# Moving the input loads of a hybrid block from ScalarE to SyncE, behind a small store

## The chip, the cores and the metric

The kernel runs on one core of a Trainium2 chip, in one launch. The metric is device time in microseconds (us). Times are given as the median of several runs with the lowest and the highest. Beside these there is one profiled execution, of which a trace shows each instruction of the engines: TensorE (PE, with its weight loads as PEld), VectorE (DVE), ScalarE (ACT), GpSimd (POOL) and SyncE (SP). An engine works off its own instructions in order and waits for others through semaphores. ACT and SP also issue DMA transfers, and these issues stand in the same order as the engine's other instructions. They appear in the trace as ACTq and SPq.

## What is computed

Four stages follow each other, each on its layer norm and with a residual sum. `x` is [4, 1024, 256] in float32.

```python
x = x + lru(_layernorm(x))     # linear recurrence over 1024 steps, then a two-layer GELU block and a layer norm
x = x + ffn(_layernorm(x))     # two gated branches, each keeps the 32 largest of 256 softmax scores per token
x = x + attention(_layernorm(x))  # 8 heads of 64, keys and values from a latent of 64
x = x + ffn(_layernorm(x))     # the same weights again
```

In `lru`, `u = einsum(x, W_in) + b_in` gives a real, an imaginary and an output part. The complex state `h[t] = lam * h[t-1] + gamma * u[t]` is scanned over time, and `out = Re(h) W_mid[0] - Im(h) W_mid[1] + o`. Then comes `y = gelu(out w1) w2 + out`, and its layer norm with gain `ln_g` and base `ln_b`. In `ffn`, a grouped convolution, batch norm, GELU and a linear layer give the logits; the weight matrix is `w_ffn`, the linear layers are `lin_t` with biases `linb`.

## The kernel before

The 4096 tokens stand in eight blocks of 512 (`NBLK`), two blocks per batch. Block `k` is one tile of 128 partitions by 4 by 256, 512 KB, and stays in SBUF for the whole kernel: `load_x` (L1040) fills it by one DMA. Two blocks of one batch hold its even and odd time steps, so that a scan runs over 512 columns.

The LRU stage (L1064 to L1116) is written out by hand:

- `lru.head` (L357) normalizes a block: statistics on DVE (L133, L134), a row of small DVE operations for the inverse root (L55 to L66, L136), scaling on ACT (L145), transposes on PE (L147), and a split into a rounded part on ACT and a rest on DVE (L160, L161). The results are the `xnt` tiles.
- `lru.tables` (L230) makes the sine and cosine tables by doubling, with one half on ACT (L272, L273) and the sums on DVE (L269 to L275).
- `lru.states` (L381) multiplies (`pu`, L170), evicts on ACT (`u`, L390) and scans on DVE (L402 to L416).
- `lru.output_weights` (L310) prepares the output weights: `gw` on ACT (L316), `pm` on PE (L320, L323), a split (L160, L161).
- `lru.outputs` (L422) makes `po` (L170, L437), evicts it as `ot` on ACT (L438), multiplies `pz` (L443), applies GELU on ACT (`zt`, L446), multiplies again (L452), adds on DVE (L455), transposes (`py`, L465), takes statistics and normalizes (`ly`, `yn` on ACT at L474); the gain, base and residual run on POOL (L472 to L484).
- `f1.head` (L501) is the head of the first feed-forward stage, with transposes and the convolution `pc` (L529). It stores turned inputs `tt` to DRAM through SP (L527), the first of them at 134.79 us.

A scheduler sets the order of instructions on each engine from the dependencies. `tc.issue_after(ins)` adds an edge for order without a wait: what is traced in the block stands behind `ins` on the engine of `ins`. A wait comes only from data. Each DMA is given one of eight semaphores in turn, and an issue waits until the DMA that had the same semaphore before is done.

The loads before the change: SP issues blocks 0 and 1. ACT issues the vector constants, the LRU weights (L217 to L225), and, behind instructions of its own, blocks 2 and 3 (behind `lru.xnt_first`, the first cast of `xnt`), `brow` (gain and base, behind the fourth eviction of `u`), and then blocks 4 to 7 together with `ffn_weights` (L984), behind the eighth eviction of `u`. `ffn_weights` loads `lint` (four DMAs), `wf` (one) and, three times in turn through one buffer, three copies of a row `v`. Each `v` is split into three bfloat16 parts by casts on ACT (L1020, L1023, L1025) and differences on POOL (L1021, L1024). The parts are `linb`, twice, and `bias`.

After the LRU stage come eight tiles of the first feed-forward stage with the attention weights (about 290 to 385 us), and then the attention stage. There score products (`sc`, L881), exponentials on ACT (L889), transposes (L900 on PE, or through DMA at L894) and value products (`pmo`, L925) of one head run beside the feed-forward tiles of later blocks. At the end, the second feed-forward stage has its own tiles (L1203).

Of the kernel before, what the change touches and what calls it, by code (L numbers as in the profile page):

```python
# [10 lines left out]
F32 = mybir.dt.float32  # L11
# [10 lines left out]
P = 128  # L22
B = 4
T = 1024
D = 256
# [3 lines left out]
NBLK = B * T // 512  # L29
# [143 lines left out]
def by_block(v):  # L173

    return [
        v[b * T : (b + 1) * T, :].rearrange("(q p r) d -> r p q d", p=P, r=CH)[r] for b in range(B) for r in range(CH)
    ]
# [796 lines left out]
def run(*gens):  # L974
    for g in gens:
        for _ in g:
            pass
# [6 lines left out]
def ffn_weights(nc, rp, cp, w, lint, lin_t, w_ffn, rows):  # L984
    vecs = w.vecs


    grp = cp.tile([P, 32], F32, tag="grp", name="grp")
    nc.gpsimd.memset(grp, 1.0)
    nc.gpsimd.affine_select(  # L990
        out=grp, in_=grp, compare_op=ALU.is_ge, fill=0.0, base=0, pattern=[[-4, 32]], channel_multiplier=1
    )
    nc.gpsimd.affine_select(
        out=grp, in_=grp, compare_op=ALU.is_ge, fill=0.0, base=3, pattern=[[4, 32]], channel_multiplier=-1
    )
    for s in range(2):
        for k in range(KD):
            nc.gpsimd.tensor_scalar(
                w.cw[:, k, s * 32 : (s + 1) * 32],
                grp,  # L1000
                vecs[:, V_CW + 2 * s + k : V_CW + 2 * s + k + 1],
                0.0,
                ALU.mult,
                ALU.add,
            )
    nc.gpsimd.memset(lint, 0.0)
    for s in range(2):
        for k in range(KD):
            r = k * 64 + s * 32
            nc.scalar.dma_start(lint[r : r + 32, s, :], lin_t[s, k * 32 : (k + 1) * 32, :])  # L1010
    nc.scalar.dma_start(w.wf, w_ffn)

    nc.gpsimd.memset(w.ones, 1.0)
    parts = [slice(32 * i, 32 * i + 32) for i in range(3)]
    for dst, at in ((w.linb[:, 0:D], 0), (w.linb[:, D : 2 * D], D), (w.bias, 4 * D)):
        v = rp.tile([P, D], F32, tag="v", name="v")
        nc.gpsimd.memset(v, 0.0)
        for i in range(3):
            nc.scalar.dma_start(v[32 * i : 32 * i + 1, :], rows[0:1, at : at + D])
        nc.scalar.copy(dst, v)  # L1020
        nc.gpsimd.tensor_tensor(v, v, dst, ALU.subtract)  # L1021
        for i in (1, 2):
            nc.scalar.copy(dst[parts[i], :], v[parts[i], :])  # L1023
        nc.gpsimd.tensor_tensor(v[parts[2], :], v[parts[2], :], dst[parts[2], :], ALU.subtract)  # L1024
        nc.scalar.copy(dst[parts[2], :], v[parts[2], :])  # L1025
# [3 lines left out]
def tile_kernel(ctx: ExitStack, tc: tile.TileContext, x_in, w_lru, vecs_in, rows, w_ffn, lin_t, w_attn, w_down, out):  # L1029
    nc = tc.nc  # L1030
# [9 lines left out]
    def load_x(engine, blk):  # L1040
        engine.dma_start(blocks[blk], by_block(x_in)[blk])
# [9 lines left out]
    w = Weights()  # L1051
    w.ident, w.vecs = ident, vecs
    w.wf = cp.tile([P, KD, D], F32, tag="wf", name="wf")
    lint = cp.tile([P, 2, D], F32, tag="lint", name="lint")
# [5 lines left out]
    f1 = Ffn("f1", tc, bp, x, w)  # L1060
# [3 lines left out]
    with ExitStack() as c1:  # L1064
        psum = Banks(c1.enter_context(tc.tile_pool(name="ps1", space=PSUM)), {"pu": 2, "po": 2, "py": 2, "pt": 2})

        brow = c1.enter_context(tc.tile_pool(name="brow", bufs=1)).tile([P, 2, D], F32, tag="brow", name="brow")
        lru = Lru(tc, c1, ident, vecs, brow, w_lru, psum)
        xb = [x[4 * k : 4 * k + 4] for k in range(NBLK)]
        xnt = [lru.head(xb[0])]  # L1070
        lru.tables(lambda: xnt.append(lru.head(xb[1])))
        with tc.issue_after(lru.xnt_first):
            for blk in range(2, 4):
                load_x(nc.scalar, blk)
        h = [[lru.states(xnt, c) for c in range(KD)]]
        lru.output_weights()
        with tc.issue_after(lru.evacuated[3]):
            nc.scalar.dma_start(brow.rearrange("p a b -> p (a b)"), rows[0, 2 * D : 4 * D].partition_broadcast(P))
        xnt += [lru.head(xb[k]) for k in (2, 3)]
        h.append([lru.states(xnt[2:4], c) for c in range(KD)])  # L1080
        for k in range(NBLK):
            last = k >= NBLK - 2
            if k == 0:
                with tc.issue_after(lru.evacuated[7]):
                    for blk in range(4, NBLK):
                        load_x(nc.scalar, blk)
                    ffn_weights(
                        nc, c1.enter_context(tc.tile_pool(name="rows", bufs=1)), cp, w, lint, lin_t, w_ffn, rows
                    )
            if k < NBLK - 1:  # L1090
                run(lru.outputs(k % CH, xb[k], xnt[k], h[k // CH], (0, 1), last))

            b = k // CH + 1
            if 2 <= b < B:
                if k % CH == 0:
                    h.append([])
                h[b].append(lru.states(xnt[b * CH : (b + 1) * CH], k % CH))
            if k + 4 < NBLK:
                xnt.append(lru.head(xb[k + 4]))
            if 2 <= k < NBLK - 2:  # L1100
                run(f1.head(k - 2, lru.sp, psum, "pt"))
        for blk in range(4, NBLK - 3):
            run(f1.head(blk, lru.sp, psum, "pt"))
        k = NBLK - 1
        ot, zt = lru.buffers()
        halves = [
            lru.outputs(k % CH, xb[k], xnt[k], h[k // CH], (i,), last, tag, [v[:, :, c : c + 256] for v in (ot, zt)])
            for i, tag, c in ((0, "pu", 0), (1, "po", 256))
        ]
        for i in (0, 0, 1, 0, 1, 0, 1, 0, 1, 1):  # L1110
            next(halves[i])
        with tc.issue_after(lru.last_gelu):
            run(f1.head(NBLK - 3, lru.sp, psum, "pt"))
        with tc.issue_after(lru.last_yn):
            run(f1.head(NBLK - 2, lru.sp, psum, "pt"))
        run(*(f1.head(NBLK - 1, lru.sp, psum, "pu", (i,), "lx", "zt") for i in range(2)))  # L1116

    with ExitStack() as c2:
# [7 lines left out]
        at = Attention(tc, x, ident, ident64, wqk, wvo, wd, sp, wp)  # L1126
        with ExitStack() as c4:
# [17 lines left out]
            first = at.prepare(0, 0, psum, "at")  # L1145
# [156 lines left out]
```

## Time and profile before

| what | us |
| --- | --- |
| median of 3 runs (lowest, highest) | 1538.0 (1536.07, 1539.59) |
| profiled execution | 1533.81 |
| its span, from first to last instruction | 1532.1 |
| idle of POOL before its first L1021, behind the cast L1020 | 57.76 |
| idle of PE before its first L443, behind `ot` L438 | 8.05 |
| idle of PE before its first L452, behind `zt` L446 | 2.08 |
| idle of PE before its second group of L465, behind `ot` L455 | 3.04 |

The mean granted clock of PE is 0.941 of full speed in this execution. Lines of the trace give the start and the length in us, the engine, the line of the kernel, the operation, its result and sources, and in brackets how long the engine was idle before it and what ended that. A "q" behind an engine's name marks the issue of a DMA; such issues are not counted as busy time. A row of several instructions is merged, and its length runs from the start of the first to the end of the last.

### The profile page before, as it was taken

What the parts mean: (1) busy time and instruction counts of PE and PEld (TensorE: products, weight loads), DVE (VectorE), ACT (ScalarE), POOL (GpSimd) and SP (SyncE); (2) the same over time, 40 slices, a digit from 0 to 9 for tenths busy, and PEclk for the clock granted to TensorE, in tenths of its full rate; (3) what the DMA queues carried; (4) which work ended last, traced back from release to release, by engine and by line L of the source; (5) the groups of instructions that cost most, each with busy time, mean ns of one, the idle gap of its engine ahead of it and who ended that gap; (6) DMA issues with size and microseconds to landing.
All of it is one profiled execution on the core that took longest, in us unless ns stands there. A gap on an engine that the chain in (4) does not pass through costs nothing. (4 is left out here: it accounts for less than half of the span.)

```text
span 1532.1 us, 28693 instructions
## 1 busy us (share of the span) xinstructions
PE 1297.4 (85%) x10136; PEld 960.2 (63%) x10136; DVE 1182.9 (77%) x3674; ACT 1014.5 (66%) x2145; POOL 681.6 (44%) x848
## 2 busy tenths in 40 slices
PE   4879998698898898898998889888999998657786
PEld 3635455365676766766776767677777776334554
DVE  8976665697878887878778687777676675499998
ACT  5353433664787777787777787877777776476664
POOL 2033333162545454544543554454443534157776
PEclk9999999698999999999999999999999999789888
DMA  3010000331454334344433345434444454000000
GB/s 117 32 41 15 21 21 14 135 101 44 76 91 90 70 70 80 67 80 77 85 76 60 65 85 81 66 60 85 78 75 88 83 95 83 1 11 24 25 25 28
DMA packets 288609, 96.51 MB, mean 63 GB/s; under 512 B 268233, under 2 KB 284626, under 8 KB 288466
## 3 DMA queue, kind: packets, MB, share of 16 engines
q1 hardware_dynamic: 283024, 88.50, 29.0%
q10 hardware_dynamic: 5442, 6.18, 1.2%
q8 instruction: 80, 1.31, 0.3%
q14 instruction: 63, 0.52, 0.1%
HBM read 16.01 MB, written 11.53 MB: 18 GB/s over the span
## 5 line engine op out<-in xcount | busy, mean ns | idle before, releaser
L893 POOL TENSOR_TENSOR pd<-pr,pd 128x1024 f16<-128x1024 f32 x128 | 273.5, 2142 | 256.5 <-ACT pd L892 198.6
L885 DVE TENSOR_REDUCE nm<-sc 128x1 f32<-128x1024 f32 x256 | 308.5, 1218 | 76.8 <-PE sc L881 75.3
L889 ACT ACTIVATE pr<-sc,nm 128x1024 f32<-128x1024 f32 x256 | 285.9, 1120 | 89.8 <-DVE nm L887 53.3
L881 PE MATMUL sc<-kh,qs 128*128 128x512 f32 x512 | 184.9, 439 | 27.1 <-ACT pr L889 19.5
L881 PE MATMUL sc<-kl,qs 128*128 128x512 f32 x512 | 162.4, 398 | 0.0
L674 DVE MATCH_REPLACE8 wk<-m,wk 128x256 f32<-128x256 f32 x384 | 158.3, 419 | 0.1
L905 ACT COPY p<-ptp 128x512 f32<-128x512 f32 x224 | 124.3, 590 | 46.3 <-PE ptp L900 38.2
L900 PE MATMUL ptp<-ident,pr 128*128 128x128 f32 x1024 | 140.2, 277 | 15.6 <-ACT pr L889 14.8
L674 DVE MAX8 m<-wk 128x8 f32<-128x256 f32 x384 | 153.0, 424 | 0.4
L925 PE MATMUL pmo<-p,la 128*64 128x128 f32 x2048 | 142.3, 287 | 5.6 <-ACT ft L524 2.9
L900 PEld LDWEIGHTS ptp<-ident,pr 128*128 128x128 f32 x1024 | 117.1, 141 | 38.0 <-ACT pr L889 24.9
L892 ACT CAST pd<-pr 128x1024 f16<-128x1024 f32 x128 | 133.3, 1055 | 5.9 <-DMA d<-pd 4.8
L925 PEld LDWEIGHTS pmo<-p,la 128*64 128x64 f32 x2048 | 121.5, 143 | 24.2 <-ACT ft L524 5.1
L881 PEld LDWEIGHTS sc<-kh,qs 128*128 128x128 f32 x512 | 85.6, 196 | 51.9 <-ACT pr L889 30.8
L881 PEld LDWEIGHTS sc<-kl,qs 128*128 128x128 f32 x512 | 97.1, 190 | 23.4 <-issue 1.4
L925 PE MATMUL pmo<-d,lb 128*64 128x128 f16 x3072 | 101.8, 221 | 7.6 <-DVE qs L853 2.5
L925 PEld LDWEIGHTS <-lb 128*64 128x64 f16 x3072 | 91.2, 111 | 25.4 <-issue 19.5
L628 POOL TENSOR_TENSOR ex<-ex,wk 128x512 f32<-128x512 f32 x61 | 77.6, 1273 | 50.8 <-DVE wk L674 41.7
L921 POOL COPY rows<-rs 128x128 f32<-128x128 f32 x128 | 36.2, 295 | 125.5 <-PE pmo L933 69.3
L936 DVE TENSOR_TENSOR on<-pmo,rb 128x128 f32<-128x128 f32 x128 | 36.5, 285 | 66.8 <-ACT rb L935 66.2
L699 PE MATMUL pf<-wf,vt 128*128 128x256 f32 x288 | 84.4, 438 | 3.6 <-ACT vt L697 3.6
L147 PE MATMUL pt<-ident,xn 128*128 128x128 f32 x256 | 48.2, 308 | 42.5 <-ACT xn L145 30.6
(306 smaller groups left out, 2789.0 us busy)
## 6 DMA issues: line engine op xcount, KB each, us to landing
tt<-ft SPq DMA_DIRECT2D x16, 256.0 KB
tt<-tt SPq DMA_DIRECT2D x8, 512.0 KB
out<-x SPq DMA_DIRECT2D x32, 128.0 KB
x<-in_x ACTq DMA_DIRECT2D x6, 512.0 KB
pf<-pfs SPq DMA_DIRECT2D x12, 256.0 KB
full<-pf SPq DMA_DIRECT2D x24, 128.0 KB
d<-pd SPq DMA_TRANSPOSE x128
wa<-in_w_attn SPq DMA_DIRECT2D x2, 640.0 KB
```

The source lines that it names most:

```text
L147: nc.tensor.transpose(pt[:, k, i * P : (i + 1) * P], xn[:, k * P : (k + 1) * P], ident)
L628: pool.tensor_tensor(ex, ex, wk, ALU.subtract)
L674: ins = make(*args).ins
L699: nc.tensor.matmul(dst, vt[:, k, :], w.wf[:, k, :], start=(k == 0 and bias is None), stop=(k == KD - 1))
L881: nc.tensor.matmul(sc[:, sl], qs[:, j, q * P : (q + 1) * P], kk[:, sl], start=(i == 0), stop=(i == 1))
L885: nc.vector.tensor_reduce(nm, sc, AX.X, ALU.max, negate=True)
L889: nc.scalar.activation(pr, sc, AF.Exp, bias=nm, accum_out=ssum[:, j : j + 1])
L892: nc.scalar.copy(pd[:, 0, :], pr)
L893: nc.gpsimd.tensor_tensor(pd[:, 1, :], pr, pd[:, 0, :], ALU.subtract)
L900: nc.tensor.transpose(pt[:, kk, :], pr[:, kc * P : (kc + 1) * P], self.ident)
L905: nc.scalar.copy(dst, pt)
L925: nc.tensor.matmul(po[j * HD : (j + 1) * HD, 0, :], v, pts[j][:, c, :], start=(n == 0), stop=(n == len(terms) - 1),)
```

## The change

All loads but the vector constants and the LRU weights are issued by SP. Their place in SP's order is set by a store of one column, 128 rows of 4 bytes, from the first `xnt` tile to DRAM. The store waits for the cast that writes this column, and the loads stand behind it in SP's order: blocks 2 and 3, `brow`, blocks 4 to 7, and the loads of `ffn_weights`. The instructions of ACT, DVE, PE and POOL stay the same in kind and number, apart from the DMA issues; the scheduler places them anew.

```diff
@@ ffn_weights
-            nc.scalar.dma_start(lint[r : r + 32, s, :], lin_t[s, k * 32 : (k + 1) * 32, :])
-    nc.scalar.dma_start(w.wf, w_ffn)
+            nc.sync.dma_start(lint[r : r + 32, s, :], lin_t[s, k * 32 : (k + 1) * 32, :])
+    nc.sync.dma_start(w.wf, w_ffn)
...
-            nc.scalar.dma_start(v[32 * i : 32 * i + 1, :], rows[0:1, at : at + D])
+            nc.sync.dma_start(v[32 * i : 32 * i + 1, :], rows[0:1, at : at + D])
@@ tile_kernel
         lru.tables(lambda: xnt.append(lru.head(xb[1])))
-        with tc.issue_after(lru.xnt_first):
+
+        gate = f1.dram.tile([P, 1], F32, tag="gate", name="gate")
+        first = nc.sync.dma_start(gate, xnt[0][0][:, 0, 0:1].bitcast(F32)).ins
+        with tc.issue_after(first):
             for blk in range(2, 4):
-                load_x(nc.scalar, blk)
+                load_x(nc.sync, blk)
+            nc.sync.dma_start(brow.rearrange("p a b -> p (a b)"), rows[0, 2 * D : 4 * D].partition_broadcast(P))
+            for blk in range(4, NBLK):
+                load_x(nc.sync, blk)
         h = [[lru.states(xnt, c) for c in range(KD)]]
         lru.output_weights()
-        with tc.issue_after(lru.evacuated[3]):
-            nc.scalar.dma_start(brow.rearrange("p a b -> p (a b)"), rows[0, 2 * D : 4 * D].partition_broadcast(P))
         xnt += [lru.head(xb[k]) for k in (2, 3)]
...
             if k == 0:
-                with tc.issue_after(lru.evacuated[7]):
-                    for blk in range(4, NBLK):
-                        load_x(nc.scalar, blk)
+                with tc.issue_after(first):
                     ffn_weights(
```

## The prediction

> **What bounds the kernel now.** I read the page first, then the stretches of time, then the timelines of the engines around the loads that the change moves.
>
> ```profile
> PE 1297.4 (85%) x10136; PEld 960.2 (63%) x10136; DVE 1182.9 (77%) x3674; ACT 1014.5 (66%) x2145; POOL 681.6 (44%) x848
> ...
> 60.00:80.00 20.00, 15.10 (x52) 9.33 (x50) 19.66 (x34) 3.11 (x4) 0.00 (x0) 0.99 0.31 104
> 80.00:100.00 20.00, 14.78 (x41) 7.38 (x42) 15.99 (x70) 10.94 (x22) 5.01 (x8) 0.84 0.08 22
> ...
> 120.00:140.00 20.00, 19.91 (x66) 10.97 (x64) 7.67 (x34) 8.86 (x16) 8.34 (x12) 0.99 0.04 14
> ```
>
> The first line is the page's busy time of each engine; the stretches list start and end, length, busy us of PE, PEld (weight loads), DVE, ACT and POOL, then granted clock, DMA share and GB/s. TensorE (PE) is the busiest engine over the span and full from 120 us on, but VectorE (DVE) fills 60 to 80 us and PE loses 5 us in each stretch from 60 to 100. The page's chain of waits begins only near 1240 us, so it says nothing of this region. The timelines of ScalarE (ACT) and PE there (start, length, what, and in brackets the idle time before it with what ended it):
>
> ```profile
> 72.57 2.05 ACTq L1041 DMA_DIRECT2D x<-in_x  x4
> 74.65 2.29 ACTq L1010 DMA_DIRECT2D lint<-in_lin_t  x4
> 76.98 0.47 ACTq L1011 DMA_DIRECT2D wf<-in_w_ffn  x1
> 77.84 4.51 ACTq L1019 DMA_DIRECT2D v<-in_rows  x3
> 82.41 1.26 ACT L438 ACTIVATE ot<-po,ob 128x512 f32<-128x512 f32 x2 [9.07 <-DMA lint<-in_lin_t]
> ...
> 83.15 5.28 PE L443 MATMUL pz<-ot,w_lru 128*128 128x512 f32 x8 [8.05 <-ACT ot L438]
> 90.50 3.70 PE L452 MATMUL pz<-zt,w_lru 128*128 128x512 f32 x8 [2.08 <-ACT zt L446]
> ...
> 94.47 0.38 PE L465 MATMUL py<-ident,ot 128*128 128x128 f32 x2
> ...
> 117.04 0.69 PE L465 MATMUL py<-ident,ot 128*128 128x128 f32 x2 [3.04 <-DVE ot L455]
> 117.38 2.91 PE L170 MATMUL po<-xnt,f 128*128 128x512 f32 x6
> ```
>
> From 72.57 to 82.4 ACT does nothing but issue twelve DMAs, and the eviction `ot` (L438) stands behind them; PE waits 8.05 us for it, then 2.08 us for `zt`. DVE at the same place:
>
> ```profile
> 19.50 1.41 DVE L133 BATCH_NORM_STATS2 lx_st<-x 128x6 f32<-128x256 f32 x4 [0.33 <-DMA x<-in_x]
> ...
> 93.45 0.75 DVE L455 SCALAR_TENSOR_TENSOR ot<-pz,vecs,ot 128x512 f32<-128x512 f32 x1 [2.21 <-issue]
> ...
> 116.24 0.74 DVE L455 SCALAR_TENSOR_TENSOR ot<-pz,vecs,ot 128x512 f32<-128x512 f32 x1
> ```
>
> DVE works from 20 us to 91.24 with no gap over 0.2 us. This is the second bound of the region: it limits how much of PE's 10 us can come back.
>
> **What the Trainium skill says.** "DMA: Bandwidth & Descriptors", section "Issuing engines are not separate DMA queues": all issuers share the 16 DMA engines, and a choice of issuer saves only the sequencer's time to initiate, "usually small". Here it isn't small: 9.8 us on ACT. "TensorE: Matmul & The Clock Gate", Part 1: an idle PE falls to half clock. The trace agrees: the granted clock is 0.50 from 80 to 86 us, and eight 512-column matmuls took 5.28 us against 3.76 us for the same eight (2 x 1.88) at 105 and 107 us. "GPSIMD Engine Reference", the table of specifications: its SBUF interface is shared with VectorE. The trace fits: the 4-column operations of DVE took 0.65 us beside POOL's 0.73 us tensor operations from 109 to 116 us, and 0.15 us elsewhere.
>
> **The change part by part.** ACT loses 21 DMA issues: two `x` at 15.8 us (hidden in its waits), `brow` (0.35 us), the twelve of 72.57 to 82.4 us, and `v` three by three at 87.6 and 94.8 us (0.84 us each). SP gains these and the store `gate`. Between the first two loads and 134.79 us SP had nothing in the trace before, so nothing but these loads themselves can be held up behind `gate`. The built program confirms the order: `gate`, x2, x3, `brow`, x4 to x7, four `lint`, `wf`, nine `v`, and `gate` waits for the first cast of `xnt` alone (L160, ends at 16.5 us).
>
> *x2 comes later.* Before, issued at 15.80, used at 19.50: 3.7 us. Now `gate` is issued at 16.5 (estimate 0.4 us, as the other issues), x2 at 17.0, so it lands near 20.7. The store's 128 rows of 4 bytes are seen nowhere in the trace: between 0 and 0.5 us in the way; I take 0.1. In the new DVE order L133 comes after two 20-column steps, so DVE waits some 1.3 us instead of 0.33. Cost 1.0 us (0.5 to 1.5), on DVE, which has no slack.
>
> *Loads against each other.* x2 to x7, `brow`, `lint`, `wf` are 3.8 MB; in the trace data flowed at 370 to 380 GB/s (18 to 20 us) and began some 1.3 us after the issue. From 18.3 us that ends near 28.5. Each load also waits on the semaphore of the DMA eight before it: `v` waits for x5, x6, x7, so its third row is issued near 28.2 and lands near 29.5. ACT reaches the first `linb` cast (L1020, before at 83.56 us) near 30 us: it now stands between the two pairs of `gw` (L316), which ran at 29.85 and 31.13. Cost 0 to 3 us, since `f` (L160) and with it DVE stand behind; I take 0. This is the cover most easily lost.
>
> *First L455.* PE and ACT alone would give 8.05 + 2.08 + 1.5 (clock, 5.28 - 3.76) = 11.6 us. But DVE's order has to be worked off: of its work up to 91.24 the three last state steps (3 x 0.6 = 1.8), a row of four aggregates (0.36) and some 22 four-column operations (2.0) now come after L455, and two splits of `xnt` (1.2) before it. 91.24 - 4.2 + 1.2 + 1.0 (x2) = 89.2 us against 93.45: **4.2 us** gained.
>
> *From there to the second L455.* PE ran without a gap from 94.47 to 113.9. Twelve transposes (L147) of the later blocks now stand before it: 3 x 0.43 = **1.3 us**. The `linb` and `bias` casts, 3 x 1.62 = 4.9 us of ACT between 83 and 101, now stand among the table steps and the first `u` evictions (30 to 50 us). The stall of **3.04 us** came since DVE's `lx` chain ran slowly beside POOL just ahead of L455; in the new order only one L133 stands between the end of the `ly` chain and L455. The six matmuls after it took 2.91 us against 1.64 at 94.61: **1.3 us** of lost clock.
>
> Sum 4.2 + 1.3 + 3.0 + 1.3 = 9.8. I keep 9, as what was late behind a removed stall often waits for the next (here ACT's `zt` and its table load). PE is full from 120 to 180 us and the order of matmuls up to 390 us differs only by transposes (L147) and `pc` (L529), so the gain is carried.
>
> *The rest.* The order of instructions is unchanged for most of the attention stage. In its first part (about 399, and 469 to 600 us) ten groups of four score matmuls (L881) now come after a block of 48 value products (L925) instead of ahead. No trace shows this order; PE idles 18 us of 460 to 620, so the ends are -5 and +5 us. I take 0.
>
> The profiled execution took 1533.81 us (span 1532.1), the median of the runs is 1538.0. 1533.81 - 9 = 1524.8; on the median, **1529.0 us**.
>
> **The rivals.**
> - *DVE takes over.* Its fullness from 20 to 91 us speaks for it; the gaps of 2.2, 1.2, 3.8 and 4.5 us that DVE has from 91 to 125 speak against. Only the first 4 us come: 1534.
> - *The gain is larger.* If the attention order also helps by 5 us: 1524. For: PE's idle time there. Against: nothing was removed there.
> - *`v` or x2 is late.* ACT waits at L1020 for 3 us or more and passes it to DVE, and little of the second half of the gain comes: about 1537, no change. For: `v` is last in 3.8 MB. Against: the rate of 370 GB/s.
> - *Slower: scores behind values.* Place: L881 from 469 to 600 us. Each of the ten groups is delayed by one block of 1.53 us (L925 x48), and with it the exponentials of ACT: 10 x 1.53 = 15.3 us, less 9, gives 1544. It decides from about 8 of 10 paid in full (8 x 1.53 = 12 = 9 + 3). Against: the block has to run anyway, and two score banks give cover.
>
> **How the numbers follow.** About 0.2% (3 us) can be told from no change. Main case, 1529 +- 4: 0.50. DVE takes over (1533 to 1535): 0.20. Larger: 0.12. Late `v`: 0.08. Slower: 0.10. So faster 0.82, same 0.08, slower 0.10. The range leaves out the slower case and the far end of the larger one: 1521 to 1537.
>
> **What will show it.** No DMA issue on ACT after 5 us; PE's wait before the first L443 under 2 us; clock near 1.00 from 75 to 90; the first L455 near 89 us; no wait of PE before the second; the DVE wait for x2 near 1.3 us and none of ACT at the first L1020; the first score matmul (378.3 us before) some 9 us earlier. It is wrong if that one is 9 us earlier and the end isn't (the attention order), or if L455 stands at 93 again (DVE).

## The result: slower by 0.4%, and the profile after

| | before | changed |
| --- | --- | --- |
| median, first five runs of each on one chip | 1536.26 | 1543.64 |
| ratio with its 95% interval | | 1.0038 (1.0027 to 1.0050) |
| profiled execution (span) | 1533.81 (1532.1) | 1542.49 (1540.8) |
| mean granted clock | 0.941 | 0.934 |
| median, a later set (50 and 17 runs) | 1537.44 | 1544.44 |
| ratio with its 95% interval | | 1.0047 (1.0033 to 1.0062) |

The five runs of the kernel before include the three of its own table. The ratios stand as recorded with their intervals; a ratio isn't the quotient of the two medians. The forecast was 1529, faster. The stretches of the changed kernel (columns as before: start and end, length, PE, PEld, DVE, ACT, POOL, then clock, DMA share and GB/s):

```profile
20.00:40.00 20.00, 9.61 (x31) 6.53 (x31) 12.07 (x54) 8.12 (x23) 1.96 (x9) 1.00 0.69 183
...
60.00:80.00 20.00, 17.37 (x58) 11.95 (x59) 20.00 (x43) 4.76 (x8) 0.00 (x0) 0.83 0.00 0
80.00:100.00 20.00, 15.38 (x43) 6.47 (x41) 20.00 (x45) 9.03 (x15) 0.00 (x0) 0.97 0.00 1
...
120.00:140.00 20.00, 20.00 (x73) 11.46 (x72) 10.24 (x47) 9.49 (x18) 10.98 (x16) 1.00 0.08 27
```

PE does gain where ACT's issues went: 15.38 us busy at 80 to 100, at clock 0.97 instead of 0.84. But DVE now has 7.9 us of idle time between 20 and 40 us, where the kernel before had none:

```profile
20.00:40.00 20.00, 16.41 (x72) 12.66 (x71) 20.00 (x110) 14.61 (x40) 1.85 (x8) 1.00 0.02 5
```

DVE's timeline of the changed kernel names the cause:

```profile
27.93 0.75 DVE L133 BATCH_NORM_STATS2 lx_st<-x 128x6 f32<-128x256 f32 x2 [8.39 <-DMA x<-in_x]
...
99.25 1.42 DVE L455 SCALAR_TENSOR_TENSOR ot<-pz,vecs,ot 128x512 f32<-128x512 f32 x2
...
119.66 0.72 DVE L455 SCALAR_TENSOR_TENSOR ot<-pz,vecs,ot 128x512 f32<-128x512 f32 x1
```

DVE waits 8.39 us for x2, where it waited 0.33. The first L455 comes at 99.25 instead of 93.45. PE at the same places:

```profile
30.69 1.22 PE L170 MATMUL pu<-xnt,w 128*128 128x512 f32 x2 [9.28 <-ACT xnt L160]
...
84.44 1.88 PE L443 MATMUL pz<-ot,w_lru 128*128 128x512 f32 x4
...
90.94 3.70 PE L452 MATMUL pz<-zt,w_lru 128*128 128x512 f32 x8 [1.04 <-ACT zt L446]
97.63 0.93 PE L147 MATMUL pt<-ident,xn 128*128 128x128 f32 x4 [2.99 <-ACT xn L145]
...
119.71 0.44 PE L465 MATMUL py<-ident,ot 128*128 128x128 f32 x2 [0.21 <-DVE ot L455]
```

The waits that the change aimed at are gone or cut: 8.05 us before L443 to none, 2.08 before L452 to 1.04, 3.04 before the second L465 to 0.21. In their stead stands one of 9.28 us at 30 us, and a smaller one of 2.99 before L147. Against the kernel before, the changed one is 8.4 us late at x2 and 1.3 us late at 121 us, and the first score matmul (L881) comes at 378.0 against 378.3: nothing gained, nothing lost up to there. The rest of the loss lies behind it. From the first to the last score matmul it is 924.1 us in this execution against 916.1, and the tail after that is 1.1 longer: -0.4 + 8.0 + 1.1 = 8.7, the difference of the spans.

**Why x2 is late.** SP issues what it should, when it should (start, length):

```profile
16.47 0.34 SPq L1074 DMA_DIRECT2D gate<-xnt  x1
16.86 0.97 SPq L1041 DMA_DIRECT2D x<-in_x  x2
17.88 0.51 SPq L1078 DMA_DIRECT2D brow<-in_rows  x1
18.43 10.18 SPq L1041 DMA_DIRECT2D x<-in_x  x4
```

x2 is issued some 0.1 us from where the prediction put it, but DVE can use it only at 27.93, 11 us after its issue, where 3.7 were expected. Stretches of one microsecond show what the DMA engines moved (last column, GB/s):

```profile
18.00:19.00 1.00, 0.32 (x2) 0.14 (x2) 1.00 (x6) 1.00 (x3) 0.00 (x0) 1.00 2.65 126
19.00:20.00 1.00, 1.00 (x4) 0.43 (x4) 0.47 (x4) 0.71 (x2) 0.00 (x0) 1.00 1.87 13
20.00:21.00 1.00, 0.32 (x3) 0.28 (x2) 0.00 (x0) 1.00 (x4) 0.00 (x0) 1.00 0.06 20
...
22.00:23.00 1.00, 0.00 (x0) 0.00 (x0) 0.00 (x0) 0.00 (x0) 0.00 (x0) 1.00 0.86 43
...
25.00:26.00 1.00, 0.00 (x0) 0.00 (x0) 0.00 (x0) 0.00 (x0) 0.00 (x0) 1.00 0.18 26
...
27.00:28.00 1.00, 0.00 (x0) 0.00 (x0) 0.07 (x1) 0.00 (x0) 0.00 (x0) 1.00 1.08 383
```

Between 19 and 26 us hardly anything flows, 13 to 49 GB/s, and then 383. The packets that move in this gap are the 1-KB packets of `x`; those of `brow` (2 KB) begin only at 28 us. The packets of 4 bytes, those of the store, stand just ahead, between 17 and 18 us. SP itself is held up too: the four issues of x4 to x7 took 2.05 us on ACT before and take 10.18 here.

So two theories stood to be tested. **The store:** `gate` blocks the loads behind it for some 7 us and eats the gain in the LRU stage. **The attention order:** the ten groups of score products that the scheduler moved cost the other 7 to 8 us. The rivals: the loads hold each other up, and the loss in attention is chance, or follows from the late LRU stage.

### The profile page after: what moved, and what is told of

It is laid out like the page before. It is cut to its first block, busy times and chain, and to the rows that moved or that the text cites. A ratio compares the mean times of both kernels' runs of the same rounds, so it can differ in the third digit from the quotient of the medians.

```text
span 1540.8 us, 28703 instructions
## 1 busy us (share of the span) xinstructions
PE 1302.6 (85%) x10136; PEld 964.7 (63%) x10136; DVE 1170.9 (76%) x3674; ACT 1013.8 (66%) x2145; POOL 682.3 (44%) x848
## 5 line engine op out<-in xcount | busy, mean ns | idle before, releaser
L881 PE MATMUL sc<-kh,qs 128*128 128x512 f32 x512 | 185.7, 440 | 25.2 <-ACT pr L889 17.4
L881 PE MATMUL sc<-kl,qs 128*128 128x512 f32 x512 | 163.7, 400 | 0.0
L674 DVE MATCH_REPLACE8 wk<-m,wk 128x256 f32<-128x256 f32 x384 | 154.0, 404 | 0.2
L674 DVE MAX8 m<-wk 128x8 f32<-128x256 f32 x384 | 147.6, 409 | 0.4
L881 PEld LDWEIGHTS sc<-kh,qs 128*128 128x128 f32 x512 | 86.7, 197 | 50.1 <-ACT pr L889 27.8
L881 PEld LDWEIGHTS sc<-kl,qs 128*128 128x128 f32 x512 | 98.0, 192 | 23.4 <-issue 1.4
L147 PE MATMUL pt<-ident,xn 128*128 128x128 f32 x256 | 50.3, 320 | 48.4 <-ACT xn L145 35.4
L699 PE MATMUL pf<-wf,vt 128*128 128x256 f32 x288 | 80.7, 420 | 2.9 <-ACT vt L697 2.7
```

The costliest lines, as they stand in the source:

```text
L147: nc.tensor.transpose(pt[:, k, i * P : (i + 1) * P], xn[:, k * P : (k + 1) * P], ident)
L674: ins = make(*args).ins
L699: nc.tensor.matmul(dst, vt[:, k, :], w.wf[:, k, :], start=(k == 0 and bias is None), stop=(k == KD - 1))
L881: nc.tensor.matmul(sc[:, sl], qs[:, j, q * P : (q + 1) * P], kk[:, sl], start=(i == 0), stop=(i == 1))
```

## The experiments

Each kernel is timed beside runs of the kernel before on the same chip. There were three chips, on which the median of the kernel before was 1535.84 (whole rows, one row, before with the gate, fifth eviction), 1536.70 (rows apart, 32 rows, two gates, sixth and seventh) and 1537.44 (changed again, one row again, x2 and x3 back on ACT); the ratio allows for this, a comparison of medians across chips doesn't. The table gathers all; the column "order" says whose order of instructions TensorE has in the attention stage. A is the order of the changed kernel. It differs from B, that of the kernel before, mainly at 398 to 415 and at 468 to 612 us. "Near B" has the order of A in the first of these stretches and that of B in the second; from some 790 us on it differs from both in places. The kernels marked B also differ from the kernel before in three small exchanges between 790 and 1050 us, and in the second feed-forward stage. Waits and places come from one profiled execution each. "Half" is the time at half clock, first in the 240 us from the first score matmul on, then up to the last one.

| kernel | order | wait for x2 | first score | first to last score | half, 240 us | half, stage | median (runs) | median less first score | ratio (interval) |
| --- | --- | --- | --- | --- | --- | --- | --- | --- | --- |
| before | B | 0.33 | 378.3 | 916.1 | 11.8 | 35.7 | 1537.44 (50) | 1159 | 1 |
| changed, first set | A | 8.39 | 378.0 | 924.1 | 21.1 | 55.2 | 1543.64 (5) | 1166 | 1.0038 (1.0027 to 1.0050) |
| changed, again | A | 9.76 | 380.3 | 918.4 | 22.0 | 39.1 | 1544.44 (17) | 1164 | 1.0047 (1.0033 to 1.0062) |
| gate of whole rows | A | 1.21 | 371.8 | 924.9 | 21.8 | 55.9 | 1536.70 (22) | 1165 | 0.9988 (0.9973 to 1.0003) |
| rows apart | A | 2.19 | 372.0 | 926.2 | 21.9 | 56.0 | 1538.48 (1) | - | - |
| 32 rows | A | 5.30 | 375.2 | 917.4 | 21.0 | 38.1 | 1533.18 (1) | - | - |
| gate of one row | B | 0.41 | 372.1 | 921.4 | 14.8 | 52.4 | 1530.42 (8) | 1158 | 0.9941 (0.9917 to 0.9966) |
| the same, again | B | 0.49 | 370.9 | 922.4 | 15.8 | 53.3 | 1530.43 (18) | 1160 | 0.9960 (0.9945 to 0.9974) |
| two gates of 64 rows | near B | 7.34 | 375.3 | 919.1 | 14.8 | 38.7 | 1536.93 (13) | 1162 | 1.0003 (0.9987 to 1.0018) |
| x2, x3 back on ACT | near B | 1.02 | 380.2 | 918.8 | 10.9 | 38.2 | 1538.95 (22) | 1159 | 1.0011 (0.9998 to 1.0024) |
| before with the gate | B | 9.07 | 378.8 | 916.1 | 15.8 | 39.7 | 1537.48 (22) | 1159 | 1.0003 (0.9988 to 1.0019) |
| before, fifth eviction | A | 0.97 | 366.8 | 917.7 | 21.1 | 38.2 | 1532.99 (17) | 1166 | 0.9960 (0.9939 to 0.9980) |
| before, sixth and seventh | near B | 0.39 | 367.8 | 917.6 | 10.9 | 38.2 | 1525.18 (6) | 1157 | 0.9925 (0.9910 to 0.9940) |

The last column but one is the key to it: from the first score matmul to the end, the order A takes 1164 to 1166 us in the median, B and near B 1157 to 1162, whatever the LRU stage did. It is a rough measure, as it takes a median of many runs less a place from one profile; the two profiles of the changed kernel differ by 2.3 us in that place. The profiles alone don't show the difference: their stages of 916.1 to 919.1 us and those of 921.4 to 926.2 both have kernels of either order.

### The store alone: whole rows

```diff
-        gate = f1.dram.tile([P, 1], F32, tag="gate", name="gate")
-        first = nc.sync.dma_start(gate, xnt[0][0][:, 0, 0:1].bitcast(F32)).ins
+        gate = f1.dram.tile([P, P], F32, tag="gate", name="gate")
+        first = nc.sync.dma_start(gate, xnt[0][0][:, 0, 0:P].bitcast(F32)).ins
```

> The gate stores whole rows: 128 rows of 512 bytes instead of 128 rows of 4 bytes. All engines keep the order of the changed kernel, the attention stage included. Theory 'small store': the 4-byte rows hold up what stands behind them. Then the wait of VectorE for x2 falls from 8.4 us to under 3, the first score matmul comes 5 to 9 us before 378.0, and the time is about 1543.6 - 7 = 1536.5, as the attention order still costs its part. Rival 'loads on SP hold each other up' (x2 and x3 with brow behind): x2 still comes 7 to 9 us late, the time stays at 1543 to 1545.

DVE's timeline of this kernel:

```profile
20.75 0.75 DVE L133 BATCH_NORM_STATS2 lx_st<-x 128x6 f32<-128x256 f32 x2 [1.21 <-DMA x<-in_x]
...
92.69 1.40 DVE L455 SCALAR_TENSOR_TENSOR ot<-pz,vecs,ot 128x512 f32<-128x512 f32 x2
```

A store of 128 times as many bytes costs 7.2 us less: the wait falls from 8.39 to 1.21, the first score matmul comes 6.2 us earlier, the median falls by 7 to 8. The loads don't hold each other up to any like extent. As the order on all engines is that of the changed kernel, this is the store and nothing else.

### What in the store costs

Apart: the rows of 4 bytes are kept, each at the head of its own 512 bytes.

```diff
-        gate = f1.dram.tile([P, 1], F32, tag="gate", name="gate")
-        first = nc.sync.dma_start(gate, xnt[0][0][:, 0, 0:1].bitcast(F32)).ins
+        gate = f1.dram.tile([P, P], F32, tag="gate", name="gate")
+        first = nc.sync.dma_start(gate[:, 0:1], xnt[0][0][:, 0, 0:1].bitcast(F32)).ins
```

> The gate still stores 128 rows of 4 bytes, but each into the head of a 512-byte row of its own, so the written bytes lie 512 bytes apart instead of side by side. The order of all engines is that of the changed kernel. Theory 'same stretch of memory': writes of 4 bytes into one and the same 512 bytes take turns; apart, they don't, and VectorE's wait for x2 falls from 8.4 us to about the 1.2 us of whole rows. Rival 'each small write is slow by itself': the wait stays at 6 to 9 us.

Fewer: 32 rows, side by side.

```diff
-        gate = f1.dram.tile([P, 1], F32, tag="gate", name="gate")
-        first = nc.sync.dma_start(gate, xnt[0][0][:, 0, 0:1].bitcast(F32)).ins
+        gate = f1.dram.tile([32, 1], F32, tag="gate", name="gate")
+        first = nc.sync.dma_start(gate, xnt[0][0][0:32, 0, 0:1].bitcast(F32)).ins
```

> The gate stores 32 rows of 4 bytes instead of 128, side by side as in the changed kernel, with the order of all engines unchanged. Theory 'a price for each row': (8.4 - 1.2) / 128 = 0.056 us a row, so 32 rows cost 1.8 us and VectorE waits about 3.0 us for x2. Rival 'a fixed price of a small store': the wait stays near 8 us.

DVE's timeline, first apart, then with 32 rows:

```profile
21.81 0.75 DVE L133 BATCH_NORM_STATS2 lx_st<-x 128x6 f32<-128x256 f32 x2 [2.19 <-DMA x<-in_x]
```

```profile
25.00 0.76 DVE L133 BATCH_NORM_STATS2 lx_st<-x 128x6 f32<-128x256 f32 x2 [5.30 <-DMA x<-in_x]
```

Rows set apart cost about 1.0 us (2.19 - 1.21), side by side 7.2. So most of the price comes with small rows that lie side by side, not with their small size by itself; at which distance it ends wasn't tried. It isn't proportional to the rows: 32 of them cost 4.1 us (5.30 - 1.21) where 1.8 was expected, 0.13 us a row, against 0.056 with 128. Neither theory had that, and why stays open. The Trainium skill, "DMA: Bandwidth & Descriptors", Specifications, says that below 512 bytes the DMA engines read, modify and write. This alone would hold for the rows set apart as well, which cost 1.0 us. The other 6.2 us fit such writes taking turns on one stretch of memory, but no run shows the engines' steps. These two kernels ran once each, so they speak by their waits and not by their times.

### Who is held up

The loads x2 and x3 alone go back to ACT, which issues them behind the same cast, ahead of the gate.

```diff
+        with tc.issue_after(lru.xnt_first):
+            for blk in range(2, 4):
+                load_x(nc.scalar, blk)
...
         with tc.issue_after(first):
-            for blk in range(2, 4):
-                load_x(nc.sync, blk)
```

> The changed kernel with x2 and x3 alone given back to ScalarE, which issues them behind the same cast as before (15.8 us), so some 0.7 us ahead of the gate and not behind it. The gate of 128 rows of 4 bytes stays, with brow, x4 to x7 and the weights behind it. Theory 'the store holds up what is queued behind it': VectorE waits under 2.5 us for x2, the first score matmul comes 4 to 8 us before 378, and as the attention order is that of the kernel before for most of it, the time is 1528 to 1534. Rival 'the store's writes slow all transfers of that time': x2 still comes 6 to 9 us late and the time is 1536 or more.

DVE's timeline:

```profile
20.14 1.41 DVE L133 BATCH_NORM_STATS2 lx_st<-x 128x6 f32<-128x256 f32 x4 [1.02 <-DMA x<-in_x]
...
28.27 1.08 DVE L133 BATCH_NORM_STATS2 lx_st<-x 128x6 f32<-128x256 f32 x3 [5.70 <-DMA x<-in_x]
...
34.25 1.08 DVE L133 BATCH_NORM_STATS2 lx_st<-x 128x6 f32<-128x256 f32 x3 [2.53 <-DMA x<-in_x]
```

x2 comes in time, but the 8 us don't go away: 5.70 us of them fall on x3, whose issue on ACT began 0.3 us ahead of the gate's on SP, and 2.53 on x4. The first score matmul is at 380.2 and the time is no better than before. The theory that the store holds up what is queued behind it was wrong, and with it the expectation of 1528 to 1534: x3 was issued by another engine and ahead of the store. The rival, that it slows all transfers of that time, comes nearer, though x2, 0.7 us ahead of the store, got through. The Trainium skill, "DMA: Bandwidth & Descriptors", "Issuing engines are not separate DMA queues", says that the DMAs of all issuers run on the same 16 DMA engines. This agrees: a store of SP holds up a load of ACT, here by 5.70 us.

### The store added to the kernel before

```diff
+        gate = f1.dram.tile([P, 1], F32, tag="gate", name="gate")
+        first = nc.scalar.dma_start(gate, xnt[0][0][:, 0, 0:1].bitcast(F32)).ins
-        with tc.issue_after(lru.xnt_first):
+        with tc.issue_after(first):
```

> The kernel before with the 128 rows of 4 bytes as its only addition: ACT issues the store just ahead of x2 and x3, all other loads stay on ACT in their places. The attention order is that of the kernel before. Theory 'small store': VectorE waits 7 to 9 us for x2 where it waited 0.33; as VectorE is full up to 91 us, 3 to 8 us of it reach the end: 1539 to 1544. Rival 'loads on SP hold each other up': x2 comes at most 1 us later, 1536 to 1537.5.

DVE's timeline:

```profile
29.39 0.75 DVE L133 BATCH_NORM_STATS2 lx_st<-x 128x6 f32<-128x256 f32 x2 [9.07 <-DMA x<-in_x]
```

DVE waits 9.07 us for x2, a little more than expected, and the second L465 comes 6.7 us late. Yet the end doesn't move, and here the expectation failed. The lag is 4.5 us at the end of the LRU stage and 0.5 at the first score matmul. DVE of the kernel before has gaps of 2.2, 1.2, 3.8 and 4.5 us between 91 and 125 us, which can take up part of it, and up to the first score matmul PE has 52.5 us at half clock in this execution against 59.8. How much is due to either wasn't shown. So a delay at 20 us need not be a delay of the end. With the changed kernel's loads the same store costs 6.2 us at the first score matmul: there it takes the room that the change had just won.

### The attention order, with the LRU stage early

A gate of one row of 512 bytes makes the scheduler keep the attention order of the kernel before, but for the small exchanges named above.

```diff
-        gate = f1.dram.tile([P, 1], F32, tag="gate", name="gate")
-        first = nc.sync.dma_start(gate, xnt[0][0][:, 0, 0:1].bitcast(F32)).ins
+        gate = f1.dram.tile([1, P], F32, tag="gate", name="gate")
+        first = nc.sync.dma_start(gate, xnt[0][0][0:1, 0, 0:P].bitcast(F32)).ins
```

> The gate stores one row of 512 bytes from one partition. The scheduler gives the attention stage the order of the kernel before, while the order of the LRU stage stays that of the changed kernel. Theory 'small store and attention order': the wait for x2 falls to under 2 us, the first score matmul comes 7 to 10 us before 378.0, and nothing is lost after it: 1526 to 1530, 8 us under the kernel before. Rival 'small store alone, the loss in attention was chance': the same time for this one and for the kernel with whole rows, 1530 to 1537. Rival 'loads hold each other up': 1535 to 1538, since only the attention order comes back.

> The kernel with a gate of one row of 512 bytes and the attention order of the kernel before, once more for more runs and a second profile. Theory 'attention order': the median stays at 1528 to 1533, under that of the kernel with whole rows (1536.7), whose LRU stage ends at the same time. Rival 'chance': 1534 to 1538.

Both sets give 1530.4. The first score matmul stands as early as with whole rows (372.1 and 370.9 against 371.8), so the 6.3 us between 1536.70 and 1530.4 come after it. In the profiled executions little of this is seen, for both fell at the upper end of this kernel's times (1534.08 and 1533.82, of 1525.8 to 1537.2); this pair rests on the timed runs. Their means, on the same chip, are 1535.1 and 1530.1 for whole rows and the first set of one row, and the intervals of these two ratios lie apart.

### The attention order, with the loads of the kernel before

Blocks 4 to 7 and the weights of the feed-forward stage behind the fifth eviction of `u`, all on ACT:

```diff
-                with tc.issue_after(lru.evacuated[7]):
+                with tc.issue_after(lru.evacuated[4]):
```

> The kernel before with one edit: blocks 4 to 7 and the weights of the feed-forward stage are issued (by ACT, as before) behind the fifth eviction of u instead of the eighth. No gate. From the first score matmul on TensorE has exactly the order of the changed kernel. Theory 'attention order': the LRU stage ends within 2 us of the kernel before, and from the first to the last score matmul 5 to 8 us are lost, which gives 1541 to 1544. Rival 'chance of the clock': attention takes the same 915 us as before, the time is 1535 to 1538.

The blocks behind the sixth, the weights behind the seventh:

```diff
-                with tc.issue_after(lru.evacuated[7]):
-                    for blk in range(4, NBLK):
+                with tc.issue_after(lru.evacuated[5]):
+                    for blk in (4, 5, 6, 7):
                         load_x(nc.scalar, blk)
+                with tc.issue_after(lru.evacuated[6]):
                     ffn_weights(
```

> The kernel before with its loads moved within ScalarE alone: blocks 4 to 7 behind the sixth eviction of u, the weights of the feed-forward stage behind the seventh, instead of both behind the eighth. No gate. TensorE has the order of the kernel before through nearly all of the attention stage. Theory 'the LRU gain comes from issues that fall into idle time of ScalarE, and the attention order decides what is left of it': the first score matmul comes 8 to 11 us before 378 as in the kernel with the fifth eviction, and the time is 1525 to 1529. Rival 'attention order doesn't matter': 1531 to 1534, as that kernel.

The expectation of the first was wrong in its time: the first score matmul doesn't come as before but 11.5 us earlier, and of this gain 2.9 us reach the end in the median (1535.84 to 1532.99 in its set), 6 by the ratio. The two differ since its times lie in two groups, six of 17 at 1522.4 to 1527.2 and the rest at 1532.0 to 1537.7. Its profile is of the first group and shows no loss of 5 to 8 us, but 1.6. The second kernel gains 10.5 us at the first score matmul and keeps them: 1525.18, ratio 0.9925, the best of all kernels here. These two kernels have the same loads on the same engine and are 1 us apart at 370 us. At the end they are 5.4 us apart by their ratios and 8.7 by their medians, each against the kernel before on its chip. The order of attention lies between them, and the second has no slow group in its six runs.

ACT of the second kernel shows why no second queue was needed:

```profile
63.65 0.78 ACT L390 ACTIVATE u<-pu,gb,par_o 128x512 f32<-128x512 f32 x1 [2.04 <-PE pu L170]
63.66 2.05 ACTq L1041 DMA_DIRECT2D x<-in_x  x4
70.74 0.78 ACT L390 ACTIVATE u<-pu,gb,par_o 128x512 f32<-128x512 f32 x1 [6.31 <-PE pu L170]
70.75 1.76 ACTq L1010 DMA_DIRECT2D lint<-in_lin_t  x4
72.55 0.44 ACTq L1011 DMA_DIRECT2D wf<-in_w_ffn  x1
```

The four issues of 63.66 lie in the 6.31 us in which ACT waits for PE anyway.

### The changed kernel's store with the order of the kernel before

```diff
-        gate = f1.dram.tile([P, 1], F32, tag="gate", name="gate")
-        first = nc.sync.dma_start(gate, xnt[0][0][:, 0, 0:1].bitcast(F32)).ins
+        gate = f1.dram.tile([64, 1], F32, tag="gate", name="gate")
+        first = nc.sync.dma_start(gate, xnt[0][0][0:64, 0, 0:1].bitcast(F32)).ins
+        gate2 = f1.dram.tile([64, 1], F32, tag="gate2", name="gate2")
+        with tc.issue_after(first):
+            first = nc.sync.dma_start(gate2, xnt[0][0][64:128, 0, 0:1].bitcast(F32)).ins
```

> The changed kernel with the gate in two stores, rows 0 to 63 and rows 64 to 127, one behind the other, so still 128 rows of 4 bytes. The scheduler now gives TensorE the order of the kernel before from the first score matmuls to two thirds of the attention stage; after that a third order. Theory 'the store costs in the LRU stage, the attention order in the attention stage': VectorE waits 7 to 9 us for x2, the first score matmul stands within 2 us of 378, and little is lost after it: 1535 to 1539. Rival 'the loss of the attention stage comes from the late LRU stage or from chance': 1542 to 1545, as the changed kernel.

DVE's timeline:

```profile
28.41 0.43 DVE L133 BATCH_NORM_STATS2 lx_st<-x 128x6 f32<-128x256 f32 x1 [7.34 <-DMA x<-in_x]
```

The late x2 is there, and the time is 1536.93. The first score matmul comes at 375.3 us, a little earlier than the 376 to 380 expected, and behind it about half of the loss is gone (1162, against 1164 to 1166 with A and 1159 before). In the kernel before with the gate x2 is late as well, and this part stays at 1159. Together they say that a late LRU stage doesn't cause the loss.

### What the order does

Stretches of 120 us, two of the kernel before and two of the changed kernel (the clock is the third number from the right):

```profile
498.00:618.00 120.00, 106.11 (x1113) 84.56 (x1114) 93.21 (x244) 92.44 (x186) 56.84 (x61) 1.00 0.39 70
...
978.00:1098.00 120.00, 107.49 (x1088) 86.48 (x1089) 85.19 (x204) 92.87 (x183) 56.33 (x58) 1.00 0.40 73
```

```profile
498.00:618.00 120.00, 105.98 (x1074) 85.24 (x1073) 87.48 (x230) 89.90 (x184) 56.29 (x60) 0.96 0.45 76
...
978.00:1098.00 120.00, 107.52 (x1064) 86.94 (x1062) 86.77 (x205) 90.06 (x177) 53.08 (x55) 0.96 0.38 72
```

PE is busy the same time, but does 39 and 24 matmuls fewer in it, at clock 0.96 instead of 1.00. PE of the changed kernel in the first of these:

```profile
508.02 0.62 PE L881 MATMUL sc<-kl,qs 128*128 128x512 f32 x2
509.07 0.27 PE L685 MATMUL pf<-bias,ones 128*128 128x256 bf16 x1 [0.43 <-ACT ex L615]
510.96 0.50 PE L170 MATMUL pf<-wf,vt 128*128 128x256 f32 x2 [1.61 <-ACT vt L160]
511.95 1.22 PE L170 MATMUL pf<-wf,vt 128*128 128x256 f32 x4 [0.49 <-DVE vt L161]
512.97 2.55 PE L170 MATMUL pmy<-wvo,onp 128*128 128x256 f32 x12
```

and of the kernel before:

```profile
511.50 0.62 PE L881 MATMUL sc<-kl,qs 128*128 128x512 f32 x2
513.38 1.09 PE L900 MATMUL ptp<-ident,pr 128*128 128x128 f32 x8 [1.26 <-ACT pr L889]
514.23 0.71 PE L881 MATMUL sc<-kh,qs 128*128 128x512 f32 x2
514.77 0.62 PE L881 MATMUL sc<-kl,qs 128*128 128x512 f32 x2
515.24 0.28 PE L685 MATMUL pf<-bias,ones 128*128 128x256 bf16 x1
515.28 0.96 PE L170 MATMUL pf<-wf,vt 128*128 128x256 f32 x6
```

With the score products in between, the chain of the feed-forward tile (`ex`, `vt`) is done when PE comes to `pf`. In the changed order PE stands there three times within 3.3 us, 2.53 us in all, and the clock is halved from 511.7 to 515.1: twelve `pmy` products take 2.55 us instead of 1.60. In the 240 us from the first score matmul on, PE is at half clock for 21 to 22 us in all six profiled executions with this order, and for 10.9 to 15.8 in the seven others timed here. All six are 6.2 to 7.4 us behind the kernel before by the score matmul that the latter has at 600 us, both counted from the first one.

But this does not decide the end. In three of the six (the changed kernel again, 32 rows, fifth eviction) nearly all of it is won back, and the stage takes 917.4 to 918.4 us, as with B. What goes with a long stage is the half clock over the whole of it: 35.7 to 39.7 us in the eight profiles of 916.1 to 919.1 us, and 52.4 to 56.0 in the five of 921.4 to 926.2. Both profiles of one row, with order B, are among these five.

The granted clock on record for each timed run says the same for the spread within a kernel: in the fast group of the fifth eviction it is 0.942 to 0.948, in the slow one 0.935 to 0.941. It doesn't explain all that lies between the orders. At 0.943 or more the means of the fifth eviction and of the sixth and seventh are equal (1524.2 and 1524.4 us, five and four runs). But whole rows and one row have nearly the same median clock (0.934; 0.9335 and 0.935), and at 0.931 to 0.934 their means are 1537.0 and 1532.3 (13 and 11 runs). So the order costs time, in part by more runs of low clock and in part at the same clock; how it does the latter stays open. The orders of the other engines change with that of PE, and no run here tells them apart.

### The changed kernel again

> The changed kernel once more, unchanged, for more runs of it. Theory 'its attention order meets the half clock in most runs': the other kernels with this order have two groups of times 8 us apart (1527 to 1531 and 1535 to 1538 with whole rows), the upper one in about 7 of 10 runs. So the median stays at 1542 to 1545 and some runs lie near 1535. Rival 'the first five runs were unlucky': the median falls to 1538 or less.

1544.44, with one run of 17 at 1537.29 and the rest from 1542. The profiled execution was that one run. It lost 7 us against the kernel before from the first score matmul to 600 us and won back 5 by 850; the first profile of the changed kernel won back less, and lost 4 more from 1030 to 1090, where three stretches are at half clock. Over the attention stage the half clock makes up 39.1 us here and 55.2 there. With whole rows there are likewise two groups of times, 1527 to 1531 (5 runs) and 1535 to 1538 (17). The Trainium skill, "TensorE: Matmul & The Clock Gate", Part 1, "What's actually happening", says that the window by which the clock is granted is 3413 ns long and runs free of the kernel; the half-clock stretches in these traces last 3.4 us or multiples of it, but for those that the end of the kernel cuts off. That a free window decides which group a run falls into would fit, but wasn't shown.

## Why the prediction was wrong

*x2 comes later* is the first step that failed. The issue (17.0, measured 16.86) was right. "The store's 128 rows of 4 bytes are seen nowhere in the trace: between 0 and 0.5 us in the way; I take 0.1" was wrong: they cost 7.2 us on DVE and 6.2 at the first score matmul. The bounds came from the length of other issues, and no row of the trace had many small writes to one place in it. A resource that no trace shows should have had an end as wide as the gain it stood against.

*Loads against each other.* With a store that doesn't block, ACT waits 1.8 us for `v` and runs the first L1020 at 31.35 (1.6 us and 38.36 in the changed kernel); three waits of DVE behind ACT (`f`, `xnt`, `st`) then sum to 1.9 us, of which `v` can be the cause at most. Inside "0 to 3", but 0 was taken.

*First L455.* 89.2 was forecast, 99.25 came. With whole rows it is 92.69, so 0.8 us of the 4.2 would have come. The missing 3.5 us have two sources. The 22 four-column operations (2.0 us) that were to move behind L455 didn't: with whole rows 74 of them (L55 to L66 and L136) stand ahead of it, before 73. And up to 1.9 us are the waits just named. DVE is otherwise full up to there, and in that the rival "DVE takes over" was right.

*From there to the second L455.* The stall of 3.04 us went, as did the wait before L443, no issue stands on ACT, and the clock from 75 to 90 us is 1.00: these signs came as given. With whole rows the gain grows from 1.0 us at the first L465 to 3.4 at the second, 2.4 where 4.3 was reckoned, and to 5.2 by 124 us, 1.8 where the clock was to give 1.3. It isn't carried evenly from there: with whole rows 3.3 us are left at 270 us, and the order of PE up to 390 us differs by more than L147 and L529, in small exchanges at 172 and from 321 to 364 us. Of the 9 taken for the first score matmul there are 6.5 with whole rows, and 0.3 with the store of the change. For the LRU stage the rival "`v` or x2 is late" came nearest, by its x2; the wait of 3 us for `v` that it named is 1.6.

*The rest: "I take 0".* This is the second step that failed. "-5 and +5 us" was too narrow, and the middle was wrong: the order costs 5 to 9 us (5.0 by the means and 6.3 by the medians of whole rows and one row, 5.4 by the ratios and 8.7 by the medians of the other pair). It alone takes the forecast gain: with whole rows, where the store no longer holds up x2, the kernel is no faster than before (0.9988). With both put right, by the gate of one row, the gain is 0.4 to 0.6%, 6 to 9 us where 9 were forecast. The slower rival named the place, the ten groups of L881, and its 1544 is what was measured, but that is luck. It reckoned ten delays of 1.53 us less 9 us gained. What happened is no gain at all at the first score matmul, since the store took it, and a smaller loss behind it. The sign given for this case, a first score matmul 9 us earlier with no earlier end, didn't show, as the first failed step hid it.

## What to carry to other kernels

A store that serves only as a wait still writes: give it one contiguous row, for 128 rows of 4 bytes side by side held up the loads near them for 7 us. Before loads are moved to another engine, look for idle time on the one that has them; issuing them there one and two evictions earlier gave 0.9925 here without a gate. An edit that leaves a scheduler free changes the order far from where it is made: compare the stage with the largest share of the time as well. Where the times of a kernel fall into two groups, one profile shows one of them: take many runs, and look at which group the profile is of.

## What the runs showed that was not expected

- The four DMA issues of x4 to x7 took 10.18 us on SP behind the store, and 2.05 us on ACT in the kernel before.
- 128 stores of 4 bytes side by side held up loads for 7.2 us, 32 for 4.1, and 128 spaced by 512 bytes for 1.0. The zero is the wait with 128 rows of 512 bytes.
- At one place, waits of 2.5 us in all within 3.3 us went with a stretch of 3.4 us at half clock that began in the last of them; twelve 256-column products took 2.55 us in it instead of 1.60.
- The times of one and the same kernel (whole rows, fifth eviction) fell into two groups some 8 us apart, the slower one with the lower granted clock.
